# A decoder layer on one core: block 6's attention, its output projections and three reciprocals are put in other places

## The chip, the cores and the metric

The kernel runs on one core of one Trainium2 chip. The metric is the device time of one execution in microseconds (us); the number for a kernel is the median of its runs. The core has a matrix engine (TensorE, PE in the profile; its weight loads are PEld), a vector engine (VectorE, DVE), a scalar engine (ScalarE, ACT), GpSimd (POOL), and SyncE (SP), which here issues nearly all DMAs. Each engine takes its instructions in the order of the program, so an instruction that waits holds up all that stand behind it on its engine.

## The reference

One pre-norm decoder layer on x of (2, 2048, 512) with a context of (2, 154, 512), in float32:

```
x = x + linear_attention(layernorm(x))       # 16 heads of 32, 128 features: elu(q@P)+1, elu(k@P)+1
x = x + cross_attention(layernorm(x), ctx)   # 16 heads, softmax over 154 keys, biases
x = x + ffn(layernorm(x))                    # 8 experts, top 6 by a softmax router, and a shared MLP
```

In the linear attention, out = (qf @ kv) * z with kv = sum of kf x v over the tokens, and z = 1 / (qf @ sum(kf) + 1e-8) for each token and head; then out @ w_out + b_out. In the cross attention the scores are softmaxed over the keys, multiplied with v, and projected by Wo.

## The kernel before, in words

The 4096 tokens are 8 blocks of 512 (nblk = 8); blocks 0 to 3 are the first batch element, 4 to 7 the second (bpb = 4). A block's 512 columns are 4 chunks of 128 (NC = 4), its tokens 4 tiles of 128 (NT = 4). Products that need full precision are three products of rounded halves (hi and lo), so that one projection of a tile or chunk is 12 matmuls ("products").

The stages, in the program's order:
- Key stage (line 1323 and on): key features (`key_features`, `key_values`) of all blocks, and in its second half, beside them, the query features (`query_features`) of blocks 0 to 3, their numerators (times kv) and denominators (times the sum of features).
- Query stage (L1359 to L1402): 16 steps n, for the chunks of blocks 4 to 7, and a 17th, each with four query features and, one step later, `numerators` and `denominators`. Beside them stands the rest of the linear attention of blocks 0 to 6.
- Score stage (L1406 to L1467): 128 steps (b, c, t); k = 4c + t counts within a block. `scores` makes score pairs (tile psc, two heads of 154 keys), their maxima on VectorE (nb, L707), exponentials on ScalarE (xe, L710), sums' reciprocals (sm) and the scaling on GpSimd (L715). `turn` transposes them three steps later (xpt, tail), `values` multiplies with v (pc).
- Expert stage: everything after that.

The rest of the linear attention of a block b runs so: `denominators` of its last chunk calls `reciprocals(b)` (L529): the denominators go to DRAM (dd), come back turned (z, L541), VectorE takes their reciprocal (L544, held in program order), and they are stored (zd, L545). `load_reciprocals(b, c)` (L555) spreads zd over the heads' rows into a tile zr for two chunks, by four DMAs. `attended(b, c)` (L565) multiplies a chunk's numerators with it on GpSimd (num, L570), rounds it on ScalarE (at, L571) and takes the rest on VectorE (L118). `attention_out(b, t)` (L574) is the projection by w_out of one tile (po_a, 12 products), by `out_tile` (L311): it loads x into a tile xr_a, GpSimd adds the bias (L319), VectorE adds the product (L322), and it is stored to x1 8 products later (L323). `cross_out` does the same for the cross attention with w_o (po_x, xr_x).

Two things set the order of the work around the change.

First, a queue named `dense` (class at L175). Products wait in it as generators; every step of a stage takes a number of them by `dense.fill` (14 twice a step at the end of the query stage, L1382; 9.5 a step in the score stage for block 0, L1447), and so fills TensorE beside the step's own work. `dense.after(n, do)` runs `do` when n products more have been taken. The three timers that the change touches or that lie near: `turned` after 10 and `stored` after 26 (24 for the last block) behind a block's reciprocals.

Second, the compiler's scheduler (L1641), which orders the instructions of every engine from the program's order and its own estimate of times; so what the program says is not quite the order on the engine.

Buffers that matter: 4 PSUM banks ("sc") are shared by key features, query features and scores; 4 others ("ps") by all else. Five SBUF tiles ("xs") serve, in turn, the layer norm's tiles of x1 (xsx), the tiles xr_a and xr_x, and the tiles of w_out and w_o as they are split (`split_weight`, L126: rounding on ScalarE, L138; rest on VectorE and GpSimd, L118).

In the query stage a table `ahead` (L1362) says which reciprocals are loaded before which step, and which `attended` run in it: steps 1 to 12 for blocks 0 to 5 and, in steps 15 and 16, block 6 (nblk - 2). The score stage's first steps (L1413 to L1428) hold `load_reciprocals` (k = 3 and 5) and `attended` (k = 4 to 7) of block 7, and at k = 0 twenty parts are put into `dense`, in the order of a string of letters: L and T are the values and the transposes of block 1's layer norm, q its four query chunks for the cross attention (`cross_query`, L668), a the outs of block 6 and b those of block 7.

Of the kernel before, what the change touches and what calls it, by code (L numbers as in the profile page):

```python
# [37 lines left out]
def decoder_layer(  # L38
# [28 lines left out]
    nblk = tokens // TB  # L67
    bpb = nblk // batches
# [149 lines left out]
    dense = Dense()  # L218
# [45 lines left out]
    def layernorm(d, b, at, xts, name, loaded=None):  # L264


        made = {}

        def values(t):
            if t == 0:  # L270
                xts[b] = new_xt(f"{name}{b}")
            tile = load_tile(d, at, t, f"{name}{b}_") if loaded is None else loaded[:, t]
            made[t] = normalize(tile, f"{name}{b}_{t}")
            yield from ()

        def turn(t):
            transposed(made.pop(t), xts[b], t, f"{name}{b}_{t}")
            yield
            yield

        return [values(t) for t in range(NT)], [turn(t) for t in range(NT)]
# [43 lines left out]
    x1 = [dram.tile([TB, D], F32, name=f"x1_{b}") for b in range(nblk)]  # L325
# [14 lines left out]
    for t in range(NT):  # L340
# [5 lines left out]
        b = nc.vector.tensor_tensor(lo, pt, hi.bitcast(F32), ALU.subtract)  # L346
# [182 lines left out]
    def reciprocals(b, pd):  # L529

        den = half(f"den{b}")
        nc.vector.tensor_scalar(den, pd, Z_EPS, None, ALU.add)
        dd = dram.tile([4, NC, TB], F32, name=f"dd{b}")
        for h in range(4):
            nc.sync.dma_start(out=dd[h], in_=den[h * HD : h * HD + NC, :])
        z = small.tile([P, H * TB // P], F32, tag="z", name=f"z{b}", bufs=1)
        flat = "h c n -> (h c n)"
        zd = dram.tile([4, NC, TB], F32, name=f"zd{b}")

        def turned():  # L540
            nc.sync.dma_start(out=z, in_=dd.rearrange(flat).rearrange("(p n) -> p n", p=P))  # L541

        def stored():
            tc.keep_in_program_order(nc.vector.reciprocal(z, z))  # L544
            nc.sync.dma_start(out=zd.rearrange(flat).rearrange("(p n) -> p n", p=P), in_=z)  # L545

        dense.after(10, turned)
        dense.after(26 if b < nblk - 1 else 24, stored)
        zds[b] = zd

    def load_numerators(b):
# [3 lines left out]
    def load_reciprocals(b, c):  # L555
        two = pair_of(f"zr{b}_{c}").bitcast(F32)
        for h in range(4):
            nc.sync.dma_start(
                out=two[h * HD : (h + 1) * HD],
                in_=zds[b][h : h + 1, c : c + 2].to_broadcast([HD, 2, TB]),  # L560
            )
        for i in range(2):
            zrs[b, c + i] = two[:, i]

    def attended(b, c):  # L565

        if c == 0:
            ats[b] = [eight([P, NC, TB], FR, f"at{b}_{i}") for i in range(2)]
        at = nums[b][:, c]
        nc.gpsimd.tensor_tensor(at, at, zrs.pop((b, c)), ALU.mult)  # L570
        nc.scalar.copy(ats[b][0][:, c], at)  # L571
        low(ats[b][1][:, c], at, ats[b][0][:, c])
# [80 lines left out]
    def load_values(bt):  # L653
        vbd = vbp.tile([P, NC, len(pairs), HD], F32, tag="vbd", name=f"vbd{bt}")
        nc.gpsimd.memset(vbd, 0.0)
        for i, (h, _, r0, r1, key) in enumerate(pairs):
            nc.sync.dma_start(
                out=vbd[r0:r1, :, i, :],
                in_=vd[bt][key : key + r1 - r0].rearrange("k (c h d) -> k c h d", c=NC, h=4)[
                    :, :, h, :  # L660
                ],
            )
        vbds[bt] = vbd
# [695 lines left out]
    wout = split_weight(w_out, "wout")  # L1359
    steps = chunks[bpb * NC :]  # L1360

    ahead = {n if n < 13 else n + 2: ((n - 1) // 2, (n - 1) % 2 * 2) for n in range(1, 15)}  # L1362
    for n in range(len(steps) + 1):
        if n < len(steps):
            b, c = steps[n]
            if n + 1 < len(steps):
                load_queries(*steps[n + 1])
        if n + 1 in ahead:
            load_reciprocals(*ahead[n + 1])
        if n == 7:  # L1370
            ln, tr = layernorm(x1[0], 0, 0, qts, "x")
            dense.add(*ln[:3])
            ln = ln[3:]
        if n == 8:
            dense.add(*tr[:1], *ln, *tr[1:])
        if n == 11:
            dense.add(*(cross_query(0, i) for i in range(NC)))
        for i in range(2):
            if n < len(steps):
                query_features(b, c, 2 * i)  # L1380
                query_features(b, c, 2 * i + 1)
            dense.fill(fl(2 * n + i, 13 if n < 12 else 14))  # L1382
            if n in ahead:
                attended(ahead[n][0], ahead[n][1] + i)
                if ahead[n][1] and i:
                    whole = ahead[n][0]
                    if whole < nblk - 2:
                        dense.add(*attention_outs(whole))
                    if whole + 1 < bpb:
                        load_numerators(whole + 1)  # L1390
            if n and i:
                columns.batch()
                numerators(*steps[n - 1])
                denominators(*steps[n - 1])
        if n == 10:
            xwq = split_weight(wq_t, "xwq")
        if n == 11:
            open_early.clear()
            attending.close()
            res = attending.enter_context(tc.tile_pool(name="res", bufs=1))  # L1400
            for i in range(NC):
                load_keys(0, i)  # L1402
# [4 lines left out]
    for n in range(len(steps) + LAG + 1):  # L1407
        if n < len(steps):
            b, c, t = steps[n]
            k = NT * c + t  # L1410
            dense.until(xsts, (b, c))
            scores(b, c, t)
            if b == 0:  # L1413
                if k == 0:
                    load_values(0)
                if k in (NC - 1 + 0, NC + 1 + 0):
                    load_reciprocals(nblk - 1, k - 0 - NC + 1)
                if NC + 0 <= k < 2 * NC + 0:
                    attended(nblk - 1, k - NC - 0)
                if k == 8:  # L1420
                    bor = load_row(bo, "bor")
                    xwo = split_weight(wo_t, "xwo")
            if b == 0 and k == 0:
                ln, tr = layernorm(x1[1], 1, 0, qts, "x")
                outs = [[attention_out(nblk - i, t) for t in range(NT)] for i in (2, 1)]
                new = [cross_query(1, i) for i in range(NC)]
                kinds = {"L": ln, "a": outs[0], "T": tr, "b": outs[1], "q": new}
                dense.add(*(kinds[x].pop(0) for x in "LLLaTLTaTTaaqbqbqbqb"))  # L1428
            if k == LAG + 0 and b:
                outs = [cross_out(b - 1, i) for i in range(NT)]  # L1430
                new = [cross_query(b + 1, i) for i in range(NC)]
                if b + 1 < nblk:
                    ln, tr = layernorm(x1[b + 1], b + 1, 0, qts, "x", xs1.pop(b + 1))
                    kinds = {"L": ln, "o": outs, "T": tr, "q": new}
                    dense.add(*(kinds[x].pop(0) for x in "LLLoTLTTToqoqoqq"))
                else:
                    dense.add(outs[0], tr[0], ln[3], outs[1], *tr[1:])
            if b == nblk - 1 and k == 1:
                ln, tr = expert_ahead(0)
                dense.add(*ln[:3])  # L1440
                load_unit(0)
            if b == nblk - 1 and k == 9:
                ln, tr = expert_ahead(1)
                ready = products(0)
                dense.add(prepare(0, 0), *ln[:3], tokens_part(0, 0), tokens_part(0, 1))
                dense.add(tr[0], ready[0], ln[3], *tr[1:], ready[1], *outs[2:])
            dense.fill(fl(k, 9.5 if b == 0 else 7.75 if b < nblk - 1 else 5.5))  # L1447
            if k == 8 and b + 2 < nblk:
                xs1[b + 2] = load_block(x1[b + 2], f"x1_{b + 2}")
            if b % bpb == bpb - 1 and b + 1 < nblk and c > 0 and t == 1:  # L1450
                load_keys(b // bpb + 1, c - 1)
            if b % bpb == 0 and b and k == 0:
                load_keys(b // bpb, NC - 1)
        if LAG <= n < len(steps) + LAG:
            turn(*steps[n - LAG])
        if n > LAG:
            b, c, t = steps[n - LAG - 1]
            if t == NT - 1:
                values(b, c)
                if c == NC - 1 and (b + 1) % bpb == 0 and b + 1 < nblk:  # L1460
                    load_values((b + 1) // bpb)
# [183 lines left out]
```

## Time and profile before

| | us |
|---|---|
| median of 3 runs | 2317.7 (2314.31 to 2324.51) |
| the profiled execution: its time | 2318.24 |
| its span, first to last instruction | 2316.5 |
| TensorE busy in the span | 2226.9 |
| VectorE busy in the span | 1682.5 |
| GpSimd, ScalarE busy in the span | 1231.5, 1103.5 |
| mean granted TensorE clock | 0.989 |
| 430 to 640 us: TensorE busy of 210; DMA share | 186.76; 0.93 |
| 640 to 760 us: TensorE busy of 120; DMA share | 105.96; 0.64 |

How to read it: a line of the page or of a timeline names the engine, the line of the kernel, the operation and out<-in by the program's names without their numbers. In a timeline the first two columns are the start and the duration in us; what stands in brackets is the idle time of the engine just before and what ended it. A window is one stretch of time with the busy time of each engine in it, then the granted clock of TensorE (1.00 is full), the mean busy share of the 16 DMA engines, and GB/s. The matmuls are pipelined, so TensorE's busy time includes overlap. The span is 1.74 us shorter than the execution's time; the rest lies around it. The key stage is over at about 495 us in this execution, the score stage begins at 640 (its first psc), and the last `values` of block 0 run at about 718.5.

### The profile page before, as it was taken

What the parts mean: (1) busy time and instruction counts of PE and PEld (TensorE: products, weight loads), DVE (VectorE), ACT (ScalarE), POOL (GpSimd) and SP (SyncE); (2) the same over time, 40 slices, a digit from 0 to 9 for tenths busy, and PEclk for the clock granted to TensorE, in tenths of its full rate; (3) what the DMA queues carried; (4) which work ended last, traced back from release to release, by engine and by line L of the source; (5) the groups of instructions that cost most, each with busy time, mean ns of one, the idle gap of its engine ahead of it and who ended that gap; (6) DMA issues with size and microseconds to landing.
All of it is one profiled execution on the core that took longest, in us unless ns stands there. A gap on an engine that the chain in (4) does not pass through costs nothing.

```text
span 2316.5 us, 35269 instructions
## 1 busy us (share of the span) xinstructions
PE 2226.9 (96%) x11978; PEld 1729.3 (75%) x11978; DVE 1682.5 (73%) x2733; ACT 1103.5 (48%) x2598; POOL 1231.5 (53%) x1084
## 2 busy tenths in 40 slices
PE   7999999898989999989999999999999999999999
PEld 5888777555666777766787877888878888788887
DVE  6554565568586877768978767787797887877777
ACT  4555677656466777765343343222433223432221
POOL 5545433446475665544866454555484554755443
PEclk9999999999999999999999999999999999999999
DMA  6556777899975666566867647566557566575553
GB/s 212 177 172 178 204 220 213 231 261 274 245 226 147 188 191 172 155 183 215 298 237 258 223 182 294 224 225 239 188 190 274 225 235 236 194 282 205 209 191 132
DMA packets 199986, 498.24 MB, mean 215 GB/s; under 512 B 27450, under 2 KB 47290, under 8 KB 179870
## 3 DMA queue, kind: packets, MB, share of 16 engines
q1 hardware_dynamic: 196446, 483.60, 63.1%
q0 software_dynamic: 3360, 12.38, 1.8%
q8 instruction: 96, 1.57, 0.3%
q14 instruction: 84, 0.69, 0.1%
HBM read 351.30 MB, written 144.60 MB: 214 GB/s over the span
## 4 chain that ended last, share of the span: by engine, by line
PE 73%; DMA 12%; DVE 6%; issue 4%; POOL 3%; ACT 2%; SPq 1%; POOLq 0%; DVEq 0%; ACTq 0%
PE pg L1099 29%; PE pf L1212 11%; PE pf L148 4%; PE pk L148 3%; PE pv L148 3%; PE po_x L148 3%; PE pq L148 3%; PE xpq L148 3%; PE pp L409 2%; PE pc L752 2%; PE xpt L732 2%; PE psc L700 1%; PE pkv L230 1%; DMA x<-xr_x 1%; DMA qst<-qd 1%
## 5 line engine op out<-in xcount | busy, mean ns | idle before, releaser
L1099 PE MATMUL pg<-xo,wq 128*128 128x512 f32 x3360 | 821.9, 392 | 3.2 <-DVE u L1113 1.5
L1099 PEld LDWEIGHTS pg<-xo,wq 128*128 128x128 f32 x3360 | 628.6, 188 | 142.8 <-DVE u L1113 3.0
L414 POOL TENSOR_TENSOR kacc<-kacc,e_k 128x512 f32<-128x512 f32 x128 | 166.1, 1298 | 228.3 <-DVE e_k L373 205.5
L1233 DVE TENSOR_TENSOR sum<-sum,pf 128x512 f32<-128x512 f32 x376 | 252.3, 683 | 44.4 <-PE pf L1212 40.5
L710 ACT ACTIVATE xe<-psc,nb 128x154 f32<-128x154 f32 x512 | 196.2, 411 | 80.6 <-DVE nb L707 72.2
L715 POOL TENSOR_TENSOR xe<-xe,sm 128x616 f32<-128x616 f32 x128 | 155.6, 1226 | 79.8 <-DVE sm L714 70.4
L1212 PE MATMUL pf<-ht,wdo 128*128 128x512 f32 x696 | 185.7, 393 | 5.3 <-DVE sum L1233 5.3
L1162 POOL TENSOR_TENSOR u<-u,gr 128x512 f32<-128x512 f32 x48 | 63.6, 1325 | 210.7 <-DVE u L1131 210.0
L373 DVE SCALAR_TENSOR_TENSOR e_k<-pp,e_k 128x512 f32<-128x512 f32 x128 | 87.4, 685 | 107.0 <-ACT e_k L372 101.1
L1212 PEld LDWEIGHTS pf<-ht,wdo 128*128 128x128 f32 x696 | 130.1, 188 | 35.8 <-DVE sum L1233 7.1
L1130 ACT ACTIVATE u<-u 128x512 f32<-128x512 f32 x80 | 50.6, 633 | 206.5 <-DVE u L1119 206.5
L1212 PE MATMUL pf<-hb,wdo 128*128 128x512 f32 x522 | 146.7, 397 | 0.0
L148 PE MATMUL pf<-wd,hp 128*128 128x512 f32 x528 | 134.0, 401 | 5.2 <-DVE mv_n L248 3.4
L707 DVE TENSOR_REDUCE nb<-psc 128x2 f32<-128x308 f32 x256 | 112.4, 467 | 29.0 <-PE psc L700 28.6
L148 PEld LDWEIGHTS pf<-wd,hp 128*128 128x128 f32 x528 | 99.4, 190 | 34.1 <-issue 6.5
L1119 DVE TENSOR_TENSOR u<-u,pg 128x512 f32<-128x512 f32 x160 | 108.4, 681 | 11.1 <-PE pg L1099 9.9
L710 ACT ACTIVATION_READ_ACCUMULATOR xe<-psc,nb 128x1 f32 x512 | 115.4, 225 | 0.0
L1212 PEld LDWEIGHTS pf<-hb,wdo 128*128 128x128 f32 x522 | 97.2, 188 | 23.0 <-DVE sum L1233 1.7
L371 ACT ACTIVATE e_k<-pp 128x512 f32<-128x512 f32 x128 | 76.8, 601 | 70.9 <-PE pp L409 60.7
L700 PE MATMUL psc<-xkst,xst 96*128 96x154 f32 x512 | 91.7, 287 | 9.6 <-ACT xe L710 7.9
L700 PEld LDWEIGHTS psc<-xkst,xst 96*128 96x128 f32 x512 | 77.8, 195 | 23.1 <-ACT xe L710 14.5
L409 PEld LDWEIGHTS pp<-pst,kst 96*128 96x128 f32 x512 | 75.5, 190 | 24.7 <-issue 8.9
(290 smaller groups left out, 5131.5 us busy)
## 6 DMA issues: line engine op xcount, KB each, us to landing
wq<-wqs SPq DMA_DIRECT2D x90, 1024.0 KB
wqs<-wq SPq DMA_DIRECT2D x30, 1024.0 KB
wdo<-wds SPq DMA_DIRECT2D x29, 1024.0 KB
kst<-kd SPq DMA_DIRECT2D x96, 256.0 KB
qst<-qd SPq DMA_DIRECT2D x96, 256.0 KB
xst<-xqd SPq DMA_DIRECT2D x96, 256.0 KB
wdo<-wds SPq DMA_DIRECT2D x29, 768.0 KB
kd<-khl SPq DMA_DIRECT2D x32, 512.0 KB
```

What stands on the lines that cost most here:

```text
L148: nc.tensor.matmul(dst, lhsT=a, rhs=b, start=n == 0, stop=n == len(todo) - 1)
L373: nc.vector.scalar_tensor_tensor(e, src, 0.0, e, ALU.max, ALU.add)
L409: nc.tensor.matmul(pp[:, h], lhsT=stks[b, c][:, h, rows], rhs=pst[:, head], start=True, stop=True)
L414: nc.gpsimd.tensor_tensor(acc, acc, kp, ALU.add)
L700: nc.tensor.matmul(psc[:, i], lhsT=xsts[b, c][:, h, t * P : (t + 1) * P], rhs=ksts[bt, c][:, h, :], start=True, stop=True,)
L707: nc.vector.tensor_reduce(nb[:, two], psc, AX.X, ALU.max, negate=True)
L710: nc.scalar.activation(e[:, h, :], psc[:, i], AF.Exp, bias=nb[:, h : h + 1], accum_out=sm[:, h : h + 1],)
L715: nc.gpsimd.tensor_tensor(e, e, sm.unsqueeze(2).to_broadcast([P, 4, keys]), ALU.mult)
L1099: nc.tensor.matmul(pb, lhsT=w[:, p, i, k, :], rhs=xop[:, q, k, :], start=first and m == 0, stop=m == len(todo) - 1, skip_group_check=True,)
L1119: nc.vector.tensor_tensor(dst, dst, pb, ALU.add)
L1212: nc.tensor.matmul(banks[i], lhsT=w[:, p, i * P : (i + 1) * P], rhs=t[q], start=new and m == 0, stop=m == len(TERMS) - 1, skip_group_check ...
L1233: nc.vector.tensor_tensor(dst, dst, banks[i], ALU.add)
```

## The change

It does four things:
1. The reciprocals of blocks 0, 1 and 2 (not 3) are taken, and stored, 60 products behind their denominators instead of 26.
2. Block 6 leaves the table `ahead`. Its reciprocals are loaded in the last two turns of the query stage's loop (n = 15 and 16), and its four `attended` calls stand in the score stage's steps k = 0 and 1, behind `scores`.
3. The layer norm of x1 of block 1 is created at n = 15 of the query stage, and its first three values are put into `dense` there, instead of at k = 0 of the score stage.
4. The order of the parts at k = 0 is T L TTT q a q aaa q b q bbb instead of LLL a T L T a TT aa q b q b q b q b: all transposes first, block 6's outs behind the first query chunk, three of block 7's outs last.

```diff
         dense.after(10, turned)
-        dense.after(26 if b < nblk - 1 else 24, stored)
+        dense.after(60 if b < bpb - 1 else 26 if b < nblk - 1 else 24, stored)
...
-    ahead = {n if n < 13 else n + 2: ((n - 1) // 2, (n - 1) % 2 * 2) for n in range(1, 15)}
+    ahead = {n: ((n - 1) // 2, (n - 1) % 2 * 2) for n in range(1, 13)}
...
         if n + 1 in ahead:
             load_reciprocals(*ahead[n + 1])
+        if n >= len(steps) - 1:
+            load_reciprocals(nblk - 2, 2 * (n - len(steps) + 1))
+        if n == len(steps) - 1:
+            ln, tr = layernorm(x1[1], 1, 0, qts, "x")
+            dense.add(*ln[:3])
+            ln = ln[3:]
...
                 if k == 0:
                     load_values(0)
+                if k < 2:
+                    attended(nblk - 2, 2 * k)
+                    attended(nblk - 2, 2 * k + 1)
                 if k in (NC - 1 + 0, NC + 1 + 0):
                     load_reciprocals(nblk - 1, k - 0 - NC + 1)
...
             if b == 0 and k == 0:
-                ln, tr = layernorm(x1[1], 1, 0, qts, "x")
                 outs = [[attention_out(nblk - i, t) for t in range(NT)] for i in (2, 1)]
                 new = [cross_query(1, i) for i in range(NC)]
                 kinds = {"L": ln, "a": outs[0], "T": tr, "b": outs[1], "q": new}
-                dense.add(*(kinds[x].pop(0) for x in "LLLaTLTaTTaaqbqbqbqb"))
+                dense.add(*(kinds[x].pop(0) for x in "TLTTTqaqaaaqbqbbb"))
```

The program of the changed kernel has as many instructions on each engine as that of the one before.

## The prediction

> **What bounds the kernel now.** I read the page's shares and chain first, then busy time by stage in 10 us windows, then each engine in order of time where TensorE is not full.
>
> ```profile
> PE 2226.9 (96%) x11978; PEld 1729.3 (75%) x11978; DVE 1682.5 (73%) x2733; ACT 1103.5 (48%) x2598; POOL 1231.5 (53%) x1084
> PE 73%; DMA 12%; DVE 6%; issue 4%; POOL 3%; ACT 2%; SPq 1%; POOLq 0%; DVEq 0%; ACTq 0%
> ```
>
> TensorE (PE) carries 73% of the chain, so only a place where PE waits, or runs at a lower clock, can pay. The change touches three such places. The windows (columns: busy us of PE, weight loads, VectorE, ScalarE, GpSimd; then granted clock, DMA share, GB/s):
>
> ```profile
> 440.00:450.00 10.00, 4.59 (x34) 3.45 (x22) 1.17 (x1) 5.77 (x12) 4.35 (x4) 0.87 0.99 282
> 450.00:460.00 10.00, 5.47 (x42) 2.84 (x43) 6.01 (x10) 2.98 (x6) 3.66 (x3) 0.62 0.89 278
> 640.00:650.00 10.00, 7.43 (x47) 4.81 (x45) 7.73 (x14) 4.73 (x17) 3.35 (x3) 1.00 0.99 247
> 650.00:660.00 10.00, 4.58 (x14) 3.69 (x15) 8.46 (x22) 6.24 (x30) 7.30 (x11) 0.61 0.38 87
> 720.00:730.00 10.00, 5.96 (x28) 4.94 (x25) 3.41 (x8) 4.39 (x17) 5.99 (x5) 0.70 0.20 51
> ```
>
> Place 1, 440 to 460. VectorE in order of time stands still for the third block's (b = 2) reciprocal; PE waits behind it:
>
> ```profile
> 453.38 0.55 DVE L544 RECIPROCAL z<-z 128x64 f32<-128x64 f32 x1 [12.21 <-DMA z<-dd]
> 453.85 0.63 DVE L373 SCALAR_TENSOR_TENSOR eq<-pqp,eq 128x512 f32<-128x512 f32 x1
> ```
>
> ```profile
> 454.53 0.80 PE L486 MATMUL pqp<-qst,pst 96*128 96x512 f32 x1 [9.94 <-DVE eq L373]
> ```
>
> The reciprocal is held in program order, its load z<-dd is late (DMA share 0.99), and the next query feature (eq) behind it frees the PSUM bank that PE wants. What ScalarE did meanwhile decides what is late next:
>
> ```profile
> 444.70 0.60 ACT L371 ACTIVATE e_k<-pp 128x512 f32<-128x512 f32 x1 [4.05 <-DMA dd<-den]
> 445.19 0.62 ACT L372 ACTIVATE eq<-eq 128x512 f32<-128x512 f32 x1
> ...
> 455.59 1.27 ACT L138 CAST wout_hi<-xswout 128x512 fp32r<-128x512 f32 x2 [5.77 <-DMA xswout<-in_w_out]
> 458.09 0.62 ACT L138 CAST wout_hi<-xswout 128x512 fp32r<-128x512 f32 x1 [1.23 <-DMA xswout<-in_w_out]
> 458.82 0.60 ACT L371 ACTIVATE eq<-pqp 128x512 f32<-128x512 f32 x1
> ```
>
> ScalarE has waits of its own on loads, just before and behind VectorE's.
>
> Place 2, 640 to 662, the passage from query to score stage, and place 3, 716 to 731, PE's own timeline:
>
> ```profile
> 641.66 0.45 PE L700 MATMUL psc<-xkst,xst 96*128 96x154 f32 x2 [0.74 <-DVE e_q L373]
> 643.60 1.07 PE L230 MATMUL pn<-e_q,kv 128*32 128x512 f32 x8 [1.48 <-DVE e_q L373]
> ...
> 652.40 0.71 PE L700 MATMUL psc<-xkst,xst 96*128 96x154 f32 x2 [2.65 <-ACT xe L710]
> 655.99 1.45 PE L700 MATMUL psc<-xkst,xst 96*128 96x154 f32 x4 [2.89 <-ACT xe L710]
> ```
>
> ```profile
> 725.29 0.46 PE L733 MATMUL tail<-ident,xe 128*104 128x128 f32 x1 [4.04 <-POOL xe L715]
> ```
>
> **The change part by part.** The two programs hold the same number of instructions on every engine; only their order differs, from the second half of the query features to the start of block 2's scores, and in a few swaps after that. So every cost is a wait.
>
> *Part 1, three reciprocals 60 products behind.* z0 (320.91) has no wait before it: 0. z1 has 3.20 us of VectorE wait, but PE is busy 10.00 of 10 us in 370 to 380: 0. z2 is the one that counts: PE's gap of 9.94 plus 2.6 us at half clock after it (1.3 lost) is 11.2 us in all. In the new order z2's reciprocal stands behind the first context key's split, which began at 464.09, where z (here at 453.38) is long there: no new wait, and zd2 has no reader for a block. What is late next: eq's exponential on ScalarE, at 445.19 for 0.62, was itself held by dd<-den until 444.70, so PE can resume at 446.5 at the earliest: 2.0 us of gap stay. Then ScalarE stops at the w_out casts until 455.59 as before, since those loads were issued at 446.67 ahead of SP's stop on zd2. Only the fourth tile's load (454.39, behind zd2) comes sooner, so that the cast at 458.09 follows the one at 455.59 to 456.86 directly. The eq behind it moves from 458.82 to 457.4; VectorE's eq takes 3.5 us from there (458.82 to 462.29) and ends at 461.6, and PE's pqp that needs that bank stood at 465.03: 3.4 us gained. The ends: 1.4 (ScalarE's own shift, if it stays the bound) and 9.2 (9.94 - 2.0 + 1.3, if the casts' loads come early too). I take **-3.4**, the row of the first PE instruction that waits for that cast. SP: zd0 to zd2 move behind other issues and free SP from 448.25 to 453.96, but DMA is at 0.98 to 1.07 in those slices and at 0.48 only from 454 to 456, so about 1 us more is moved there.
>
> From the Trainium skill, "Perfetto Trace Analysis", Identifying the Most-Contended Engine: improve the engine that is most occupied first; that is DMA here (though the page itself calls DMA occupancy misleading), and by it part 1 would bring only the 1.0 us of DMA time above, and the sum would be 2.4 us higher.
>
> *Part 2, block 6's attention, layer norm of block 1 and the new queue order.* The front hardly moves: VectorE's new order still has block 6's first `at` ahead of the features e_q of the last chunk, and the stores of xqd go ahead of zr6's load. I keep the 0.74 and 1.48. Lost in places 2 and 3 today: gaps 0.74 + 1.48 + 2.65 + 2.89 = 7.8; half clock while busy, 656 to 662.5, 6.3 us at half, 3.2; place 3, gaps 0.96 + 4.04 = 5.0, and 5.1 us at half clock, 2.5. Sum **18.5 us**.
> In the new order, behind the last denominators PE has 15 score pairs and 4 transposes and no product until xpq of block 1, which needs the fourth transpose's cast. Before, 24 products of block 6's outs (0.23 us each) lay among them. Score pairs run at ScalarE's pace: exponentials start 0.37 us apart, two to a pair. VectorE reaches the second tile's second maximum at about 651.4 (today 651.01; its x1 loads are no sooner, landing at 648.5); from there 11 pairs x 0.73 = 8.0, three casts 1.6, and 0.9 for VectorE's share: first product at 662. From 645 to 662 PE has 15 x 0.27 + 4 x 0.37 = 5.6 us of work, so 11.4 us idle. Then about 4 us at half clock, as after 658.3: 2.0. Place 3: the outs of block 7 now come last and together; their stores free the buffers that GpSimd's xr_x loads want, and GpSimd has three xr_x ahead of the second xe of block 1 instead of one. Between 0 and today's 7.5 I take 2.5, since PE gets there some 3 us later. Sum: 2.2 + 11.4 + 2.0 + 2.5 = **18.1**. Part 2 is thus **-0.4**: the idle time is moved, not removed. Its ends: -8 (no idle time beyond the 10 us of pacing, nothing at place 3) and +11 (today's place 3 and 6 more, see the second rival).
>
> The clock in this trace fell to 0.50 at 652.6, after a gap of 2.65 us, and rose again at 662.5. The Trainium skill, "TensorE: Matmul & The Clock Gate", Part 1, has the clock halved after about 3.4 us idle; by it evenly paced score pairs would keep the full clock, and part 2 would be 2.0 better. The row is nearer, as it is this stage's.
>
> Sum: 2318.24 (the profiled execution; span 2316.5) - 3.4 - 0.4 = 2314.4. That execution was 0.5 above the median of 2317.7, so **2314** against the median.
>
> **Rivals.**
> *The whole wait goes* (0.22). With SP not stopped at zd2 the casts' loads come sooner and part 1 brings 9.2; place 3 vanishes, part 2 brings 2.9. 2317.7 - 12.1 = 2306. For: both waits end with a DMA. Against: DMA is full from 434 to 454.
> *Slower: w_o arrives late* (0.25). In the new SP order the second w_o tile waits for the store of block 6's first out, which PE now makes at 668 instead of 648; behind it stand xqd1_0, zd7, an xst load, zr7 and the last two w_o tiles. Store 5, xqd to 9.5 (698.46), zr 4.8, again xqd: they land near 697, while ScalarE reaches the casts (682.44 today, no wait) near 690 with the next exponentials behind them. PE has products for some 3 us of it: 4 us of gap and 2 of half clock. With part 1 at its lower end: 2314 + 6 + 2 = 2322. It decides if the second pair of w_o loads is issued over 20 us after PE's first product of block 6's outs.
> *As forecast*: 0.53.
>
> **How the numbers follow.** Likeliest 2314. The forecast's own bounds are about 2308 to 2320; to leave out no more than 2 in 10, I go halfway beyond each rival: **2303 to 2326**. About 0.5% (11.6 us) is what a measurement of this kernel can tell from no change: below 2306.1 lies half of the first rival and a little of the forecast, 0.14; above 2329.3 the tail of the second, 0.08; within, 0.78.
>
> **What would show it.** Part 1: the 9.94 gap is 2 us, followed by a new one of 3 to 6 us before the pqp that stood at 465.03, with ScalarE waiting on xswout. If there is no such gap, the first rival holds. Part 2: PE nearly idle for 10 us or more at clock 0.5 with only psc and pt_x, then unbroken products; GpSimd's waits on xr_x loads shorter. ScalarE waiting on xsxwo speaks for the second rival. All from block 2's scores on should take as long as today; if it does not, the prediction is wrong in what it left out.

## The result, and the profile after

| | us |
|---|---|
| before, median of 11 runs | 2317.16 (2313.31 to 2324.51) |
| after, median of 11 runs | 2324.56 (2319.86 to 2328.94) |
| ratio after / before | 1.0025, 95% interval 1.0015 to 1.0035 |
| profiled execution after: time, span | 2324.56, 2322.8 |

The changed kernel is slower, by 0.25% or 5.8 us of the ratio (the medians are 7.4 us apart). The forecast was 2314 with a range of 2303 to 2326: the time lies inside the range and on the other side of no change, near the rival "w_o arrives late" (2322), though not for that rival's reason.

On the page of the changed kernel the shares and the engines' busy times have hardly moved; nothing there tells what happened:

```profile
PE 2232.1 (96%) x11978; PEld 1733.6 (75%) x11978; DVE 1683.2 (72%) x2733; ACT 1102.9 (47%) x2598; POOL 1230.6 (53%) x1084
PE 71%; DMA 11%; DVE 7%; POOL 3%; issue 3%; ACT 2%; SPq 1%; DVEq 0%; POOLq 0%; ACTq 0%
```

The windows of the changed kernel, in the columns of the prediction:

```profile
440.00:450.00 10.00, 10.00 (x87) 6.92 (x87) 6.92 (x10) 6.74 (x14) 7.55 (x6) 1.00 0.96 294
450.00:460.00 10.00, 5.15 (x31) 4.91 (x30) 2.76 (x5) 4.62 (x9) 2.87 (x3) 0.85 1.02 310
640.00:650.00 10.00, 5.07 (x31) 2.79 (x24) 8.25 (x19) 5.05 (x24) 2.49 (x4) 0.74 0.89 249
650.00:660.00 10.00, 7.48 (x31) 6.47 (x32) 9.10 (x23) 7.96 (x39) 10.00 (x12) 0.50 0.36 89
660.00:670.00 10.00, 10.00 (x38) 8.11 (x37) 2.61 (x6) 1.08 (x2) 4.41 (x4) 0.74 0.21 57
...
720.00:730.00 10.00, 6.59 (x35) 3.77 (x38) 3.81 (x11) 5.59 (x27) 6.84 (x6) 0.83 0.34 105
```

In these two executions place 1 (440 to 460) has improved: PE is busy 15.15 us of 20 instead of 10.06. Place 2 has become worse: from 640 to 670 PE works at clocks of 0.74, 0.50 and 0.74. Place 3 (720 to 730) is only a little better: 6.59 us busy at a clock of 0.83, where it was 5.96 at 0.70.

To add such windows up, the rest of this text uses one measure. **Loss** of a window is PE's idle time plus its busy time multiplied by (1 - granted clock); for 650 to 660 above that is 2.52 + 7.48 x 0.50 = 6.26 us. The clock of a window is its mean over the time, so this is a little rough where the clock changes inside a window. The losses below are sums over windows of 10 us. Several traces of each program are needed, since one trace scatters by some 2 us in a stage. The rows are sorted by what the program has in the score stage.

| program | 400-520 | 520-630 | 630-690 | 690-760 |
|---|---|---|---|---|
| before, three traces | 19.1, 21.0, 18.1 | 10.9, 12.3, 14.3 | 11.0, 10.2, 11.5 | 8.2, 7.9, 8.9 |
| z2_only | 15.3 | 10.4 | 10.2 | 8.7 |
| z12_only | 20.3 | 11.7 | 11.7 | 12.2 |
| z0_only, p1_alone, ln_alone | 20.6, 18.2, 18.0 | 7.6, 11.9, 10.6 | 12.9, 11.8, 11.7 | 12.3, 11.8, 11.2 |
| p2_alone, noatt | 17.1, 17.4 | 10.4, 9.9 | 15.2, 15.2 | 6.9, 10.2 |
| after, three traces | 15.7, 18.1, 19.4 | 9.9, 11.3, 8.4 | 17.1, 15.1, 16.3 | 8.1, 7.5, 8.1 |
| after_wobig | 14.2 | 12.3 | 16.9 | 5.4 |
| before_wobig, z2_wobig, z2_wobig_rep | 17.1, 15.8, 19.3 | 11.6, 8.9, 12.2 | 12.2, 11.6, 10.4 | 6.3, 6.6, 5.6 |
| after_held, z2_held, z2_held_b | 20.3, 16.7, 19.0 | 19.4, 14.3, 17.3 | 12.6, 17.5, 17.5 | 6.1, 0.8, 2.9 |

What the names mean follows. Read down the fourth column: of the programs that hold back no outs, every one with the new order of parts loses 15 to 17 us from 630 to 690, and every other 10 to 13.

### The profile page after: what moved, and what is told of

It is laid out like the page before. It is cut to its first block, busy times and chain, and to the rows that moved or that the text cites. A ratio compares the mean times of both kernels' runs of the same rounds, so it can differ in the third digit from the quotient of the medians.

```text
span 2322.8 us, 35272 instructions
## 1 busy us (share of the span) xinstructions
PE 2232.1 (96%) x11978; PEld 1733.6 (75%) x11978; DVE 1683.2 (72%) x2733; ACT 1102.9 (47%) x2598; POOL 1230.6 (53%) x1084
## 4 chain that ended last, share of the span: by engine, by line
PE 71%; DMA 11%; DVE 7%; POOL 3%; issue 3%; ACT 2%; SPq 1%; DVEq 0%; POOLq 0%; ACTq 0%
PE pg L1099 27%; PE pf L1212 12%; PE pq L148 4%; PE pk L148 4%; PE pv L148 3%; PE po_x L148 3%; PE xpq L148 3%; PE pf L148 3%; PE pp L409 2%; PE pc L752 2%; PE xpt L732 2%; PE pkv L230 2%; PE psc L700 1%; DMA x<-xr_a 1%; DMA wq<-wqs 1%
## 5 line engine op out<-in xcount | busy, mean ns | idle before, releaser
L710 ACT ACTIVATE xe<-psc,nb 128x154 f32<-128x154 f32 x512 | 196.2, 412 | 81.3 <-DVE nb L707 71.2
L710 ACT ACTIVATION_READ_ACCUMULATOR xe<-psc,nb 128x1 f32 x512 | 115.6, 226 | 0.0
```

Source lines behind the costliest of these rows:

```text
L710: nc.scalar.activation(e[:, h, :], psc[:, i], AF.Exp, bias=nb[:, h : h + 1], accum_out=sm[:, h : h + 1],)
```

## The experiments

All ratios are to the kernel before, run beside it on the same chip, with their 95% interval. The third column of a table gives the median.

### The parts by themselves

**p1_alone** is the kernel before with the changed line `dense.after(60 if b < bpb - 1 else 26 if b < nblk - 1 else 24, stored)`. 

> Only the timer of 60 products, the rest as before. Theory A (the two traces read together: part 1 gains 3.4 us by the first score pair, part 2 loses 6.9 us between 640 and 780 us): 2317.2 - 3.4 = 2313.8, with the first psc some 3.4 us earlier against the key stage, no VectorE wait on z<-dd, and places 2 and 3 with the same gaps as before. Rival B (what part 1 gains is lost again behind the passage, since the score stage's first loads come no sooner): 2317, with the first psc early and block 2's scores on time. Rival C (the 4.9 us gap that the changed kernel has at 457 us is a part of part 1 and will cost more here): 2319.

**p2_alone** is the changed kernel with the old line back, `dense.after(26 if b < nblk - 1 else 24, stored)`. 

> The changed kernel with the timer of 26 again: part 2 by itself. Theory A: part 2 costs 6.9 us by the traces (from -3.4 at 640 us to +3.5 at 780 us), and by the medians 7.4 + 3.4 = 10.8; so 2324 to 2328, with the 9.94 us gap back at 454 us and the score-only stretch as in the changed kernel. Rival B (part 1 brings nothing by the end): 2324.6, as the changed kernel. If it is at 2320 or less, the loss needs both parts together.

**ln_alone** is p1_alone with

```diff
+        if n == len(steps) - 1:
+            ln, tr = layernorm(x1[1], 1, 0, qts, "x")
+            dense.add(*ln[:3])
+            ln = ln[3:]
...
-                ln, tr = layernorm(x1[1], 1, 0, qts, "x")
...
-                dense.add(*(kinds[x].pop(0) for x in "LLLaTLTaTTaaqbqbqbqb"))
+                dense.add(*(kinds[x].pop(0) for x in "aTLTaTTaaqbqbqbqb"))
```

> Part 1, and of part 2 only the earlier layer norm of block 1; block 6's attention and the order of the outs as before (a T L T a T T a a q b q b q b q b). Theory D (the loss comes from the order of the parts: no product among the first 15 score pairs): the same as part 1 alone within 1 us, 2314. Rival E (the early layer norm's loads and buffers push the xr_a and w_o tiles back in the five shared buffers): 2317 to 2320, with PE waits on xr_a or ScalarE waits on xsxwo.

**noatt** is the changed kernel with the old `ahead` table, without the two `load_reciprocals` of n = 15 and 16, and without the `attended` of k = 0 and 1. 

> The changed kernel with block 6's attention and its reciprocals' loads back in the query stage's last two steps; the new order of the parts and the early layer norm stay. Theory D (the order of the parts is what costs): as the changed kernel, 2323 to 2326, with 10 us or more of idle PE and the clock at half between 642 and 662 us. Rival F (the attention's place costs, by GpSimd and ScalarE work and zr6's loads among the first scores): 2314 to 2317.

| program | ratio | median, us |
|---|---|---|
| p1_alone | 1.0035 (1.0021 to 1.0049) | 2329.05 |
| p2_alone | 1.0022 (1.0010 to 1.0034) | 2325.59 |
| ln_alone | 1.0026 (1.0013 to 1.0038) | 2325.96 |
| noatt | 1.0021 (1.0009 to 1.0032) | 2325.17 |
| (before beside them) | | 2320.23 |

Three things follow. Part 2 alone costs 5.1 us; at 2325.59 that is in theory A's range and as near to rival B's 2324.6, by which part 1 brings nothing, so this run doesn't tell the two apart. Part 1 alone made the kernel slower by 8 us, where theory A had 3.4 us of gain and the slowest rival, C, 2319. The parts don't add. And noatt is as slow as the changed kernel: the place of block 6's attention is not what costs (theory D against F).

ln_alone tells more than was asked of it. Its compiled program has the same instructions in the same order on every engine as p1_alone's: with the old order of the parts, creating block 1's layer norm earlier changes nothing. So rival E can't hold here, and of what part 2 does the new order of the parts is left as the cost (with the earlier layer norm, which no run takes out of that order). The two runs are two measurements of one program, and their 1.0035 and 1.0026 show how far such ratios scatter.

### What part 1 is when nothing else moves

The instruction orders of these programs show where part 1's loss comes in. Moving the **first** reciprocal (z0), which had no wait, makes the scheduler set some 130 to 140 of 10,900 PE instructions elsewhere (how many depends on how the two orders are laid side by side), most of them in the first two blocks of the score stage. Moving the third one (z2), or the second and third (z1 and z2), moves those reciprocals and their stores and nothing else. So three programs differ from the kernel before in the condition of that line only:

```diff
-        dense.after(26 if b < nblk - 1 else 24, stored)
+        dense.after(60 if b == 2 else 26 if b < nblk - 1 else 24, stored)           # z2_only
+        dense.after(60 if 0 < b < bpb - 1 else 26 if b < nblk - 1 else 24, stored)  # z12_only
+        dense.after(60 if b < 1 else 26 if b < nblk - 1 else 24, stored)            # z0_only
```

**before_again** is the kernel before, unchanged. 

> The kernel before, once more. It tells what a second execution of the same program shows. Theory G (the 9.94 us gap at 454 us belongs to the one execution that the prediction read; the program with part 2 alone, which has the same order there, showed 3.01): a gap of 2 to 6 us there, at the same total time. Theory A (the gap is what this program always has): 9 to 11 us. The ratio to the kernel before is 1.000; if it is 1.002, all the comparisons so far carry that much for nothing.

**z2_only.** 

> Only the third reciprocal (b = 2) 60 products behind; against the kernel before one VectorE instruction (the reciprocal) and one DMA (its store) stand elsewhere, and nothing else. Theory A (the prediction's part 1): -3.4 us, ratio 0.9985. Theory G: the wait is shorter in most executions, and what is gained at 455 us is lost again before the query stage (all five profiles so far gave 1.3 to 3.9 us back between 474 and 505 us): ratio 1.000, less than 1.2 us either way. Rival C (the store and the reciprocal are in the way in their new place): 1.001 or more.

**z0_only.** 

> Only the first reciprocal (b = 0) 60 products behind. It had no wait, but the move lets the compiler's scheduler set 141 of 10,916 TensorE instructions elsewhere, nearly all of them in the first two blocks of the score stage, with 75 of VectorE, 32 of ScalarE and 16 of GpSimd. Theory H (this reshuffle is what makes part 1 alone slow): ratio 1.002 to 1.0035, with 3 to 5 us more lost between 690 and 740 us than before. Rival I (the order in the score stage makes no difference; part 1 is slow by its own waits in the key stage): 1.000.

**z12_only.** 

> The second and third reciprocals (b = 1, 2) 60 products behind, the first at its old place, so that the order of everything else stays that of the kernel before: all of part 1 that had a wait, without the reshuffle that the first one sets off. z2 alone gave 0.9992 [0.998, 1.0004], which holds both the prediction's 3.4 us (0.9985) and nothing. Theory A: 0.9985 again. Theory G: 1.000. The trace: 3 to 5 us less lost between 440 and 520 us, as in z2 alone; if the total is not lower, the same 3 to 5 us are to be found elsewhere.

| program | ratio | median, us; before beside it |
|---|---|---|
| before_again | 0.9993 (0.9979 to 1.0007) | 2318.44; 2318.70 |
| z2_only | 0.9992 (0.9980 to 1.0004) | 2318.67; 2318.70 |
| z0_only | 1.0014 (1.0003 to 1.0026) | 2324.30; 2318.70 |
| z12_only | 0.9995 (0.9982 to 1.0008) | 2319.45; 2320.15 |

The same program against itself gives 0.9993, so the comparison carries no bias that could make +0.25%. The gap is no accident of one execution: before_again, VectorE and then PE:

```profile
457.74 0.55 DVE L544 RECIPROCAL z<-z 128x64 f32<-128x64 f32 x1 [11.96 <-DMA z<-dd]
```

```profile
458.89 0.79 PE L486 MATMUL pqp<-qst,pst 96*128 96x512 f32 x1 [9.70 <-DVE eq L373]
```

It isn't constant either. Over six traces with z2 at its old place it was 9.94, 9.70, 7.03, 7.75, 3.55 and, in p2_alone, 3.01:

```profile
451.81 0.79 PE L486 MATMUL pqp<-qst,pst 96*128 96x512 f32 x1 [3.01 <-DVE eq L373]
```

With z2 moved the wait is gone and another stands some 12 us further on, in z2_only 4.38 us before 458.62, with a clock of 0.50 until 463. The loss from 400 to 520 us is 18.8 on average over the six traces with z2 at its old place (17.1 to 21.0) and 17.7 over the fourteen with z2 moved (14.3 to 20.3): 1.1 us, give or take some 1.8, so neither clear of nothing nor near 3.4. In the totals even that isn't seen: z2_only and z12_only are where before_again is, and the changed kernel against p2_alone, which differ by part 1 (and one PE swap), stands at 1.0025 against 1.0022. None of these ratios alone excludes theory A's 0.9985 (z2_only reaches down to 0.9980); together they speak against it.

z0_only, p1_alone and ln_alone have one and the same order of PE instructions, and 1.0014, 1.0035 and 1.0026: the reshuffle costs between 3 and 8 us. Theory H's place for it shows too: from 690 to 760 z0_only loses 12.3 us, p1_alone 11.8, ln_alone 11.2, the kernel before 7.9 to 8.9. In GpSimd's order of z0_only the bias add for block 7's second tile (xr_a7_1) stands ahead of w_o's rests and of the scalings of three score tiles; before, it stood behind all five. It waits there for its x tile, and they with it:

```profile
680.89 0.85 POOL L289 DMA_DIRECT2D x<-x  x1
689.39 1.28 POOL L319 TENSOR_TENSOR xr_a<-xr_a,bout 128x512 f32<-128x512 f32 x1 [7.65 <-DMA xr_a<-in_x]
690.64 2.51 POOL L118 TENSOR_TENSOR xwo_lo<-xsxwo,xwo_hi 128x512 fp32r<-128x512 f32 x2
```

z12_only, whose PE order is that of the kernel before, also lost 12.2 us there in its one trace, at an unchanged median. So the size rests on the three ratios; that the place is this one is likely, not shown.

### The shared buffers

**after_wobig** loads w_o's four tiles into one large tile of another pool instead of four of the five shared "xs" buffers. **before_wobig** does the same to the kernel before, **z2_wobig** to z2_only, and **z2_wobig_rep** is z2_wobig again.

```diff
-                    xwo = split_weight(wo_t, "xwo")
+                    xwo = split_weight(load_weight(wo_t, "xwo"), "xwo")
```

> The changed kernel with the four tiles of w_o loaded into one large tile of another pool instead of four of the five shared buffers, so that the loads of block 7's x tiles need not wait for the rounding of w_o. Theory K (the losses of 690 to 740 us come from those buffers: GpSimd 3.9 us and VectorE 3.3 us idle before 698, TensorE 3.4 us before 726): GpSimd's wait on xr_a goes, that stretch loses under 4 us instead of 8, and the time is 3 to 5 us lower than the changed kernel's, ratio about 1.001. Rival L (SP's own order holds the loads, since it stands on the loads of xst that wait for the stores of xqd): the waits stay, and so does the ratio of 1.0025.

> The kernel before with the third reciprocal 60 products behind, and w_o's four tiles in one large tile of another pool instead of four of the five shared buffers. Theory K (the stretch from 690 us on is held by the shared buffers): it loses 5 us or less there instead of 8 to 12, GpSimd's 5 us waits on xr_x shrink, ratio 0.997 to 0.998, faster than both kernels. Rival L (SP's order holds the loads, since they stand behind loads of xst that wait for the stores of xqd): 8 us or more, and ratio 0.999 to 1.001.

> The kernel before with w_o's four tiles in one large tile, and nothing of part 1. z2_wobig gave 0.998 [0.9967, 0.9993]. Theory K (the buffers bring nearly all of it): 0.998 to 0.9985, and 6 to 7 us lost from 690 to 760 us instead of 8 to 9. Theory A (the moved reciprocal brings 3.4 us of it): 0.9995.

> z2_wobig once more, since it was the fastest of many: if its gain is real, 0.997 to 0.999 again; if it was the luck of one draw, 0.9995 to 1.0005.

| program | ratio | median, us; before beside it |
|---|---|---|
| after_wobig | 1.0016 (1.0005 to 1.0026) | 2322.93; 2318.70 |
| z2_wobig | 0.9980 (0.9967 to 0.9993) | 2314.45; 2319.25 |
| z2_wobig_rep | 0.9983 (0.9972 to 0.9994) | 2316.29; 2320.20 |
| before_wobig | 0.9960 (0.9947 to 0.9974) | 2313.54; 2320.20 |

z2_wobig, twice, and before_wobig beat both kernels, and before_wobig, without anything of the change, has the lowest ratio (of 5 runs only). From 690 to 760 us these three lose 5.6 to 6.6 instead of 7.9 to 8.9, and after_wobig 5.4 instead of 7.5 to 8.1, so theory K holds for some 2 us, less than it foresaw. In the changed kernel GpSimd waits for block 7's x tile, and later for x1:

```profile
697.11 1.27 POOL L319 TENSOR_TENSOR xr_a<-xr_a,bout 128x512 f32<-128x512 f32 x1 [3.85 <-DMA xr_a<-in_x]
...
722.79 2.48 POOL L319 TENSOR_TENSOR xr_x<-xr_x,bor 128x512 f32<-128x512 f32 x2 [5.87 <-DMA xr_x<-x]
```

In after_wobig the first of these is 0.33 us, and the second, 4.83 us, stays. In z2_wobig the two 5 us waits on xr_x of the kernel before (5.47 and 5.08) have become 0.79 and 2.85. First the kernel before, then z2_wobig:

```profile
722.80 1.26 POOL L319 TENSOR_TENSOR xr_x<-xr_x,bor 128x512 f32<-128x512 f32 x1 [5.08 <-DMA xr_x<-x]
```

```profile
718.88 1.27 POOL L319 TENSOR_TENSOR xr_x<-xr_x,bor 128x512 f32<-128x512 f32 x1 [2.85 <-DMA xr_x<-x]
```

The gain lies from 710 to 740: 1.9 us lost in after_wobig instead of 4.1 to 5.1, and 0.0 in the other three instead of 7.1 to 7.6. From 690 to 710 it is not better: 3.5 in after_wobig, where the changed kernel lost 2.9 to 4.0, and 5.6 to 6.6 in the three, where the kernel before lost 0.3 to 0.8. By their ratios the three gain 4 to 9 us, more than 2. The edit also moves some 110 PE instructions in the score stage (some 230 in after_wobig), so how much is the buffers and how much the new order is not separated. The moved reciprocal adds nothing to it: before_wobig does without it and is no slower.

### Filling the empty stretch

Part 2 leaves the first 15 score pairs without a product among them. **after_held** takes the last two outs of block 5 (24 products, 5.5 us) out of the query stage and puts them there; **z2_held** and **z2_held_b** do it to z2_only, whose order has the letters LLLzaTLzTaTTaaqbqbqbqb and LLLaTLzTaTzTaaqbqbqbqb.

```diff
-                        dense.add(*attention_outs(whole))
+                        dense.add(*attention_outs(whole)[: 2 if whole == nblk - 3 else NT])
...
-                kinds = {"L": ln, "a": outs[0], "T": tr, "b": outs[1], "q": new}
-                dense.add(*(kinds[x].pop(0) for x in "TLTTTqaqaaaqbqbbb"))
+                kinds = {"L": ln, "a": outs[0], "T": tr, "b": outs[1], "q": new, "z": attention_outs(nblk - 3)[2:]}
+                dense.add(*(kinds[x].pop(0) for x in "TzLTzTTqaqaaaqbqbbb"))
```

> The changed kernel with the last two outs of block 5 (24 products, 5.5 us of TensorE) held back from the query stage's last steps and put among block 1's transposes at the start of the score stage, where part 2 leaves no product. Theory M (part 2's cost is the 642 to 668 us stretch, because there is nothing to multiply): that stretch loses about 10 us instead of 15 to 17, and the time falls by some 5 us to the level of the kernel before, ratio 1.000 to 1.001. Rival N (the stretch is paced by the score pairs, and products among them only push the pairs back): the stretch loses less but the next 80 us more; ratio 1.0025 as the changed kernel, or worse.

> The kernel before with the third reciprocal 60 products behind and the same two outs of block 5 held back into the start of the score stage, which there has 24 products of block 6 already. Theory M: place 2 loses 11 us today (7.8 of gaps, 3.2 at half clock), of which 24 products fill 4 to 6: ratio 0.997 to 0.998, better than both kernels. Rival N (more products push the score pairs, block 7's outs and w_o back): 1.000 to 1.003, with longer GpSimd and TensorE waits between 690 and 740 us.

> As z2_held, with the two held outs later among the parts (one behind the first transpose, one behind the second). Theory M: as z2_held or up to 2 us better, as the products lie where the 2.65 and 2.89 us gaps were; 0.997 to 0.998. Rival N: 1.000 to 1.003.

| program | ratio | median, us; before beside them 2320.15 |
|---|---|---|
| after_held | 1.0021 (1.0008 to 1.0034) | 2324.75 |
| z2_held | 1.0023 (1.0010 to 1.0036) | 2325.92 |
| z2_held_b | 1.0031 (1.0018 to 1.0043) | 2327.93 |

after_held shows half of theory M: with products in it, the stretch from 630 to 690 loses 12.6 instead of 15.1 to 17.1. The other half fails: the products are missing where they were taken from. From 520 to 630 it loses 19.4 instead of 8.4 to 11.3, since the query stage's own waits lie bare; this trace is of the slowest of its 12 runs, but z2_held and z2_held_b also lose more there (14.3 and 17.3). PE in after_held, at the end of that stage:

```profile
599.62 0.50 PE L486 MATMUL pqp<-qst,pst 96*128 96x512 f32 x1 [2.40 <-DVE e_q L373]
...
624.89 1.94 PE L230 MATMUL pd<-e_q,ksz 128*32 128x512 f32 x8 [3.01 <-DVE xhl L676]
```

z2_held is neither M nor N: 690 to 760 falls to 0.8 us, and 630 to 690 rises to 17.5.

### Second and third traces

**before_third.** 

> The kernel before, a third trace. Loss of TensorE (idle time and the part of its busy time that the granted clock takes): two traces gave 19.1 and 22.4 us from 400 to 520, 11.0 and 10.2 from 640 to 690, 8.3 and 7.9 from 690 to 760, 11.1 and 13.1 from 1060 to 1420 us. If the expert stage's difference belongs to the change, this trace has 11 to 13 there; if it is scatter, it may have up to 16.

**after_second.** 

> The changed kernel, a second trace. The first lost 15.9 us from 400 to 520, 15.1 from 640 to 690 (and 2.0 more just before 640), 8.1 from 690 to 760, 14.3 from 1060 to 1420 us. Theory M (part 2 costs the first stretch alone): 14 to 17 again from 640 to 690, and the other stretches within 3 us of the kernel before's. The prediction's place 3 (2.5 us from 690 to 760) would show as less than 4.

**after_third.** 

> The changed kernel, a third trace: as the second. Three traces of each program then give a mean and a spread for each stretch.

Their times were 2320.97, 2325.93 and 2330.55 us, one execution each. They are in the table of losses: the stretch from 630 to 690 is 10.2 to 11.5 in three traces of the one program and 15.1 to 17.1 in three of the other, and 690 to 760 is the same in both on average to within 0.5 us. From 1050 to 1440 us, where the two programs are the same but for a few swaps at the start, the loss was 12.0, 12.6 and 13.2 before and 14.5, 14.6 and 19.3 after, 3.5 more on average. p1_alone lost 16.7 there, with no instruction in another place from block 3's scores on, and ln_alone, the same program, 11.5. So this is not put down to the order of the instructions; what it is stays open.

## Why the prediction was wrong, step by step

**Part 1, -3.4: mis-sized.** Its mechanism is as written. The gap of 9.94 us went (of the 2 us that were to stay, the three traces of the changed kernel have none, 1.38 and 0.33). A new one of 4.85 us came (5.18 and 4.62 in the other two traces), in the range of 3 to 6, though before another product than the one named, and ScalarE's waits for w_out stand just before it. The changed kernel, PE and then ScalarE:

```profile
457.74 0.62 PE L148 MATMUL xpk<-ct,xwk_hi 128*128 128x308 f32 x1 [4.85 <-DVE kf L617]
```

```profile
451.69 0.62 ACT L138 CAST wout_hi<-xswout 128x512 fp32r<-128x512 f32 x1 [3.08 <-DMA xswout<-in_w_out]
...
455.89 1.34 ACT L138 CAST wout_hi<-xswout 128x512 fp32r<-128x512 f32 x2 [3.58 <-DMA xswout<-in_w_out]
```

What failed is the size: "3.4 us gained" was measured from one trace, whose gap of 9.94 was the longest of six (mean 6.8). The traces show 1.1 us, with a scatter that reaches nothing, and the totals none. The rule of the Trainium skill that was weighed there ("Perfetto Trace Analysis", Identifying the Most-Contended Engine: the most occupied engine first) would have given 1.0 us, the DMA time alone; this case's traces are nearer to that than to the row that was preferred. A small misreading beside it: behind the gap the clock stayed at half until 457.7, 3.1 us and not 2.6, which is 0.3 us more lost.

**"z0 has no wait before it: 0" failed for a kernel with part 1 alone.** A step priced at nothing because nothing waits can still move the scheduler's order; z0_only shows 1.0014, p1_alone and ln_alone 1.0035 and 1.0026. In the changed kernel this costs no more, since part 2 gives the same stage another order anyway (p2_alone and the changed kernel have one PE swap between them).

**Part 2, today's 18.5: right.** By the measure of loss three traces have 10.9 + 8.3 = 19.2 on average.

**Part 2, place 2 (2.2 + 11.4 + 2.0 = 15.6): right in sum by luck, not in its terms.** Six traces with the new order give 16.0. But of the 17.1 in the changed kernel's first trace only 9.5 are idle time (13.6 forecast) and 7.7 half clock (2.0 forecast); over the six it is 8.4 to 9.5 and 5.8 to 7.9. Two errors of 4 to 5 us each cancel. PE in the changed kernel:

```profile
643.48 0.45 PE L700 MATMUL psc<-xkst,xst 96*128 96x154 f32 x2 [0.97 <-ACT xe L710]
644.22 0.45 PE L700 MATMUL psc<-xkst,xst 96*128 96x154 f32 x2 [0.29 <-ACT xe L710]
645.45 0.71 PE L700 MATMUL psc<-xkst,xst 96*128 96x154 f32 x2 [0.78 <-ACT xe L710]
649.02 1.45 PE L700 MATMUL psc<-xkst,xst 96*128 96x154 f32 x4 [2.86 <-ACT xe L710]
...
655.62 1.09 PE L259 MATMUL pt_x<-ident,xsx 128*128 128x128 f32 x4 [0.69 <-DVE sm L714]
```

The pairs come at the pace of the exponentials, as forecast, and the first product is at 660.44 (662 forecast). But a pair takes 0.45 us before 645 and 0.7 after it: the clock is at half for 20 us, so some two fifths of what the stretch loses is slow work, not idle time.

**Part 2, place 3 (2.5): the step that failed.** "Between 0 and today's 7.5 I take 2.5, since PE gets there some 3 us later." From 690 to 760 the three traces lose 7.5 to 8.1, as much as today. They do so in two pieces. Place 3 itself (710 to 740) lost 7.1 to 7.6 and now loses 4.1 to 5.1: some 2.8 us less, and not 5. And from 690 to 710 a loss of 2.9 to 4.0 is new (0.3 to 0.8 before), which the forecast had at nothing (z2_only and z12_only, with the old order, lose 4.0 and 6.4 there too, so the new order need not be its only cause). All that feeds this stretch comes later too: block 6's outs 10 to 12 us, w_o's casts at 689.76 instead of 682.44, and the x tiles of block 7, which are loaded into the shared buffers that w_o's tiles held, are issued from 691.76 on, behind those casts. Before, GpSimd took the bias of block 7's second and third tile without a wait:

```profile
691.27 2.55 POOL L319 TENSOR_TENSOR xr_a<-xr_a,bout 128x512 f32<-128x512 f32 x2
```

In the changed kernel VectorE stands behind GpSimd's wait of 3.85 us at 697.11, shown above, and PE behind VectorE; at place 3 PE still waits for GpSimd, 3.39 us where it was 4.04:

```profile
698.41 0.69 DVE L322 TENSOR_TENSOR xr_a<-xr_a,po_a 128x512 f32<-128x512 f32 x1 [3.34 <-POOL xr_a L319]
```

```profile
699.15 0.64 PE L733 MATMUL tail<-ident,xe 128*104 128x128 f32 x4 [1.17 <-DVE xr_a L322]
...
726.50 0.37 PE L733 MATMUL tail<-ident,xe 128*104 128x128 f32 x1 [3.39 <-POOL xe L715]
```

So a later arrival of PE gained nothing here, since the loads came later with it. That the shared buffers are the whole reason is not shown: after_wobig takes GpSimd's wait away and still loses 3.5 us from 690 to 710. With 7.6 (the changed kernel's traces and p2_alone's; 8.2 with noatt's 10.2) in place of 2.5, the sum for part 2 is 16.0 + 7.6 - 19.2 = +4.4; p2_alone measured +5.1, with 2.3 to 7.9.

**The sum.** -1.1 + 4.4 = +3.3, and 3.5 behind 1050 us that stay unexplained, against 5.8 by the ratio. The times of single instructions in the three traces of each program show where. At the key stage's last product of features and values (pkv, L230) the changed kernel is 3.1 us earlier on average. From there to block 2's first exponential (L710) the kernel before takes 284.3, 282.5 and 287.6 us and the changed one 288.3, 288.3 and 289.2: +3.8. From that exponential to the end it is 1552.9, 1553.7 and 1554.1 against 1557.3, 1558.3 and 1562.1: +5.7, though the orders there differ by a few swaps only. So "All from block 2's scores on should take as long as today" failed as well, by about as much as place 3 did, and its cause stays open. p1_alone and ln_alone are longer there too (1560.8 and 1557.4), z2_only and z12_only hardly (1554.9 and 1554.1).

**The rivals.** "The whole wait goes" failed, as the new gap of 4.85 shows. "w_o arrives late" met its own condition: the second pair of w_o loads is issued at 684.63, 23 us after PE's first product of block 6's outs at 661.46. Yet ScalarE has no wait on xsxwo in any of the three traces; what is late is the x tiles that take w_o's buffers. That rival's time was right to 3 us, its engine wrong. The rival with which the chances should have been heavier is the plain one: the stretch without products costs what was computed, and nothing is given back for it.

## What to carry to other kernels

When idle time is moved from one place to another, the place that it leaves must be shown to become faster: a wait that ends with a load whose buffer or issue depends on the moved work can move along with it. A gap that ends with a DMA should be sized from several traces, not from the one at hand. And before an edit "off the path" is priced at zero, its effect on the compiled instruction order has to be looked at, and for an experiment the variant chosen that moves only the one instruction.

## What the runs showed of the hardware that was not expected

The clock of TensorE went to half at about 644.7 us in the changed kernel after no gap longer than 1.85 us, in a stretch where PE was busy 60% of the time (5.41 of 9 us from 636 to 645), and came back at about 665.2, after 5 us without a gap. After a single long gap the delay varies: 2 us in z2_only (idle from 454.2, half from about 456.4), 5 us in before_again (449.2 and 454.2). The Trainium skill, "TensorE: Matmul & The Clock Gate", Part 1, names an idle window of about 3.4 us that runs freely; the varying delay agrees with a free-running window, and the fall in the changed kernel shows that no idle stretch of that length is needed. So evenly paced pairs didn't keep the full clock, and the preference of the row over that rule was right.

The traces show the windows themselves. In each of the twenty, all changes of the granted clock lie whole multiples of 3.413 us apart (before: 447.43, 457.67, 652.23, which the prediction read as 652.6, and 662.47). Cut along that grid from 60 us on, every window at full clock in which PE was busy less than 44% was followed by half clock, and none in which it was busy more than 82%; in between both occur, and the fall at 644.7 came after one of 62%. At half clock no window with PE busy less than 85% was followed by full clock.
